# Two attention layers on one core: inverses written and read back in separate steps, mask loads, one accumulation and two norm operations moved

## The chip, the cores and the metric

The kernel runs on one core of a Trainium2 chip. The metric is the device time in microseconds (us) of one execution; of several executions the median is taken. The engines are called as the profile calls them: PE (TensorE matmul; PEld its weight loads), DVE (VectorE), ACT (ScalarE), POOL (GpSimd) and SP (SyncE, which here only issues DMAs). Each works through its own instructions in program order and waits where an operand is not ready.

## The reference

Sixteen batches of 1024 rows of 256 numbers pass through two masked-attention layers, each with a residual. All is float32; the adjacency is int32, with about 3% ones.

```python
h = jnp.maximum(_layernorm(x, axis=-1), 0.0)
x = x + _L0_gnn_ref(h, adj, ...)      # 4 heads of 64
h = jnp.maximum(_layernorm(x, axis=-1), 0.0)
x = x + _L1_gnn_ref(h, adj, ...)      # 8 heads of 32, with biases
# in each layer, for every head:
scores = q @ k.T * scale
attn = softmax(where(adj != 0, scores, -inf))
heads = attn @ v                      # concatenated, then @ Wo.T + bo
```

The layer norm takes the mean and the variance of each row: (x - m) / sqrt(v + eps).

## The kernel before

**Steps.** The attention is a stream of 768 steps. One step covers one quarter of a group's work in layer 0 (two heads, two blocks of 128 keys, 512 queries; four steps a group) or one eighth in layer 1 (four heads, one block of keys; eight steps a group). A group is half of the heads for half of the queries (`qh`, `g`), so that a batch has four groups: 16 steps in layer 0, 32 in layer 1. The stream interleaves batches: 16 steps of layer 0 of batch b+1, then 32 of layer 1 of batch b. This unit of 48 steps is called a period here, period b, and its steps are places 0 to 47; place 0 is `a = first[b+1]` of the code, place 16 is `c = second[b]`. Places of 48 and over lie in the period after.

**One step** (`Stream.run`, line 517). PE makes the scores into two PSUM pairs of three (`scores`, line 429, matmuls on 437); two steps later it multiplies the exponentials with the values (`weigh`, 471). Between, DVE applies the mask and writes the tile `p` (453; two instructions a step), and ACT takes the exponential in place (459). In layer 1 the weighing is done at odd places for two steps together. The row sums of the softmax come from adding `p` tiles and then one multiplication with ones (`count`, 338, on PE). In layer 0 the tiles are added on DVE and POOL (`add_tiles`, 480 to 486). In layer 1 POOL adds the two tiles of a pair (572; `p` of odd steps has two buffers, so DVE waits if POOL is late), and DMAs that POOL issues add those sums (`accumulate`, 558, 1 MB each).

**What is put between.** `later(i, f)` registers work for step i; it is issued at the end of that step in each engine's queue, in the order of registration (`LARGE` ones last). A step number is thus only a position in a queue. It is not a time. `end_group` (596) registers, when a group is done (step i; place 25, 33, 41 and 49 for the four groups of layer 1, and 5, 9, 13, 17 for those of layer 0): `spread` (the row sums go from PSUM by ACT and then by small DMAs to 128 lanes, 357 and 370), `invert` (DVE reciprocal `vn`, 378; a DMA writes it to `vd` in DRAM, 380; two or four DMAs read it back, broadcast, to `inv`, 383, each waiting on SP until `vd` has landed), `normalize` (POOL multiplies the output `cat` with `inv`, 389), and after the second group `end_half` (output projection, residual and, in layer 1, storing x: 419, 424, 427).

**Masks.** Each batch has eight mask tiles of 128 rows. `Mask.load` (line 145) is a DMA that POOL issues into the one buffer `adj`; `flip` (151) is a transposing DMA that SP issues into the one buffer `adjT`; `put` (160) is an ACT instruction that packs it. In the code (lines 768 to 771) they stand at places i-6, i-3 and i, for i = 7, 12, 17, 22, 33, 37, 41, 45. A load waits on POOL for the turning before it, which reads `adj`.

**Norms.** `norms` (705) registers `stats` for half of the rows in two steps: DVE takes bn_stats and bn_aggr of two tiles at each (188, 189). After the fourth tile POOL makes `ve` (192), the power -1/2 of it (194), `less` (196) and their product (198), all of 128x4 elements; ACT then normalizes. In periods from b = 1 on, the second parts of `stats` stand at places 12, 20, 29 and 38. `place_blocks` (245) and `put_blocks` (238) are the DMAs, on SP, by which normalized rows are turned; `open_x` (132) loads x on SP at places 5 and 13.

Of the kernel before, what the change touches and what calls it, by code (L numbers as in the profile page):

```python
# [10 lines left out]
F32 = mybir.dt.float32  # L11
# [4 lines left out]
ALU = mybir.AluOpType  # L16
PSUM = bass.MemoryType.PSUM

P = 128
EPS = 1e-5  # L20
# [65 lines left out]
def fast_program(ctx, tc, a, w, loads, chk):  # L86
# [3 lines left out]
    nc = tc.nc  # L90
    x, adj, out = a["x"], a["adj"], a["out"]
# [9 lines left out]
    small = ctx.enter_context(tc.tile_pool(name="small", bufs=2))  # L101
# [69 lines left out]
    class Inputs:  # L171
# [7 lines left out]
        def stats(self, half, tiles=range(4)):  # L179
            n = f"{self.n}_{half}"  # L180
            if 0 in tiles:
                self.mv[half] = small.tile([P, 4, 2], F32, tag="mv", name=f"mv_{n}")
            mv = self.mv[half]
            for i in tiles:
                stats = small.tile(
                    [P, nc.vector.BN_STATS_DIM], F32, tag="stats", bufs=1, name=f"st_{n}_{i}"
                )
                nc.vector.bn_stats(stats, xs[self.b, half][:, i, :])
                nc.vector.bn_aggr(mv[:, i, :], stats)
            if 3 in tiles:  # L190
                ve = small.tile([P, 4], F32, bufs=1, tag="ve", name=f"ve_{n}")
                nc.gpsimd.tensor_scalar_add(ve, mv[:, :, 1], EPS)
                self.rstd[half] = small.tile([P, 4], F32, tag="rstd", bufs=3, name=f"rstd_{n}")
                nc.gpsimd.tensor_tensor(self.rstd[half], ve, w.mhalf, ALU.pow)
                less = small.tile([P, 4], F32, bufs=1, tag="less", name=f"less_{n}")
                nc.gpsimd.tensor_scalar_mul(less, mv[:, :, 0], -1.0)
                self.shift[half] = small.tile([P, 4], F32, tag="shift", bufs=3, name=f"shift_{n}")
                nc.gpsimd.tensor_mul(self.shift[half], less, self.rstd[half])

# [109 lines left out]
    class Group:  # L309
# [65 lines left out]
        def invert(self):  # L375

            vn = small.tile([P, self.n_f], F32, tag="vn", bufs=1, name=f"vn_{self.n}")
            nc.vector.reciprocal(vn, self.sn)
            vd = dram.tile([self.per, 512], F32, tag=f"vd{self.layer}", name=f"vd_{self.n}")
            nc.sync.dma_start(self.lanes(vd), vn)  # L380
            self.inv = work.tile([P, 512], F32, tag="inv", bufs=1, name=f"inv_{self.n}")
            for r in range(self.per):
                nc.sync.dma_start(
                    self.inv[r * self.D : (r + 1) * self.D, :], vd[r].partition_broadcast(self.D)
                )
# [111 lines left out]
    class Stream:  # L497
# [12 lines left out]
        def later(self, i, f, *args):  # L510
            self.due.setdefault(i, []).append((f, args))
# [48 lines left out]
        def count_steps(self, i, st):  # L560


            gr, j = st.gr, st.j
            if gr.hurry and j >= NT - 2:
                if st.last:
                    self.counted(i, gr)
                gr.count(st.p, False, st.last)
            elif j % 2:
                one = self.steps[i - LEAD - 1].p
                if not (gr.brief or gr.pairs) and j == 7:  # L570
                    self.accumulate(gr.two, gr.one)
                nc.gpsimd.tensor_add(one, one, st.p)  # L572
                if gr.pairs:
                    self.later(i + 2, gr.count, one, j == 1, st.last)
                elif j == 1:
                    gr.one = one
                elif j == 3:
                    self.accumulate(one, gr.one)
                    gr.one = one
                    if gr.brief:  # L580
                        self.later(i + 8, gr.count, one, True, False)
                elif gr.brief:
                    self.later(i + (6 if j == 5 else 4), gr.count, one, False, st.last)
                elif j == 5:
                    gr.two = one
                else:
                    self.later(i + (2 if gr.last else 3), self.accumulate, one, gr.two)
                    self.later(i + (4 if gr.last else 8), gr.count, one, True, True)

        def counted(self, i, gr):  # L590
# [5 lines left out]
        def end_group(self, i, gr):  # L596

            if gr.hurry:
                for f in (gr.spread, gr.finish, gr.inp.test):
                    self.later(i, f)  # L600
                return

            if gr.layer == 0:
                self.later(i + 4, gr.count_added)
                at = 4, 6, 8, 11
            else:
                at = (8, 12, 17, 19) if gr.qh == 0 else (8, 11, 14)
                if gr.pairs:
                    at = 2, 5, 7, 9
                elif gr.last:  # L610
                    at = 4, 7, 9, 11
            for k, f in zip(at, (gr.spread, gr.invert, gr.normalize)):
                self.later(i + k, f)
            if gr.last:

                k = 7 if gr.layer or gr.inp.b == 0 else 37
                self.later(i + k if gr.inp.b + gr.layer < B - 1 else len(self.steps) + 2, gr.inp.test)
            if gr.g == 1:
                self.later(i + at[3], gr.end_half)

    def open_w(n):
        for _ in range(n):
# [5 lines left out]
    mask, inp = masks[0], inputs[0][0]  # L628
# [74 lines left out]
    later = stream.later  # L703

    def norms(inp, half, *at, whole=False):

        for i, f in zip(at, (inp.stats, inp.stats, inp.norm, inp.norm)):
            rest = (whole,) if i in at[2:] else ()
            later(i, f, half, (0, 1) if i in (at[0], at[2]) else (2, 3), *rest)
        later(at[3] + 1, inp.add_bias, half)  # L710

    def half_inputs(inp, half, *at):

        for i, f in zip(at, (inp.turn, inp.k, inp.q, inp.values)):
            later(i, f, half)
# [13 lines left out]
    for t in range(NT):  # L729
        i = 5 + 2 * t  # L730
# [8 lines left out]
    for b in range(B - 1):  # L739
        mine, a, c = inputs[1][b], first[b + 1], second[b]  # L740
        if b == 0:

            norms(mine, 0, a + 5, a + 6, a + 8, a + 9, whole=True)
            half_inputs(mine, 0, a + 11, a + 12, a + 14, a + 14)
            norms(mine, 1, a + 13, a + 14, a + 15, c, whole=True)
            half_inputs(mine, 1, c + 1, c + 3, c + 6, c + 4)
        else:
            norms(mine, 0, a - 20, a - 19, a - 16, a - 15)
            block_inputs(mine, 0, a - 14, a - 12, a, a + 2, a + 8)
            norms(mine, 1, a - 14, a - 10, a - 8, a - 6)  # L750
            block_inputs(mine, 1, a, a + 6, c, c + 6, c + 2)
        for i, u in zip((0, 2, 4, 6, 8, 10, 12, 13), range(NT)):
            later(a + i, masks[b].second, u)
        if b + 2 < B:
            other, mask = inputs[0][b + 2], masks[b + 2]
            later(a + 5, open_x, b + 2, 0)
            later(a + 13, open_x, b + 2, 1)
            if b == 0:
                norms(other, 0, a + 14, a + 15, c + 2, c + 3)
                block_inputs(other, 0, c + 4, c + 5, c + 8, c + 16, c + 18)  # L760
                norms(other, 1, c + 3, c + 4, c + 6, c + 7)
                block_inputs(other, 1, c + 10, c + 11, c + 22, c + 26, c + 30)
            else:
                norms(other, 0, a + 10, a + 12, a + 13, a + 15)
                block_inputs(other, 0, c, c + 1, c + 8, c + 16, c + 18)
                norms(other, 1, c, c + 4, c + 5, c + 6)
                block_inputs(other, 1, c + 7, c + 8, c + 22, c + 26, c + 30)
            for i, t in zip((7, 12, 17, 22, 33, 37, 41, 45), range(NT)):
                later(a + i - 6, mask.load, t)
                later(a + i - 3, mask.flip, t)  # L770
                later(a + i, mask.put, t)
        else:
            last, e = inputs[1][b + 1], c + 32
            norms(last, 0, c + 5, c + 6, c + 8, c + 9)
            block_inputs(last, 0, c + 10, c + 11, c + 14, c + 16, c + 20)
            norms(last, 1, c + 13, c + 14, c + 16, c + 17)
            block_inputs(last, 1, c + 18, c + 19, c + 24, e + 6, e + 4)
            for u in range(NT):
                later(c + 8 + 2 * u, masks[b + 1].second, u)
# [158 lines left out]
def kernel(  # L938
# [28 lines left out]
    with ExitStack() as fast, tc.manual_schedule():  # L967
        fast_program(fast, tc, a, w, loads, chk)
# [61 lines left out]
```

## Time and profile before

| what | us |
|---|---|
| median of 3 runs | 3355.89 |
| lowest and highest run | 3343.33, 3359.55 |
| the profiled execution, its own time | 3353.67 |
| its span, first to last instruction | 3351.9 |
| PE busy (96%) | 3228.7 |
| DVE busy (73%) | 2459.4 |
| POOL busy (70%) | 2349.5 |
| ACT busy (67%) | 2256.7 |

The mean clock granted to PE is 0.981 of full speed. In the profile a row such as "PE pz L338 <- DMA p<-p" reads: PE stood idle ahead of line 338, which writes `pz`, until the DMA from `p` to `p` had landed; then the total, the times and the longest. A timeline row gives start, length, engine, line, operation, `out<-in`, shapes and, in brackets, the idle time ahead of it. "SPq" is SP's issuing queue. A busy PE isn't PE at its peak, since the ends of matmuls are modelled.

### The profile page before, as it was taken

The page shows a single profiled execution, that of the slowest core. Times are in us where ns is not written, and L with a number is a line of the kernel's source. Part 1 is how long each engine was busy: PE and PEld are TensorE (multiplying, and loading weights), DVE is VectorE, ACT ScalarE, POOL GpSimd, SP SyncE. Part 2 cuts the span into 40 slices and gives each one's busy share as a digit, 9 for nine tenths or more (in the row PEclk, how much of TensorE's full clock was granted, in tenths as well). Part 3 has the DMA queues.
Part 4 walks back from the last instruction along what each step waited for, and adds up shares of the span by engine and source line. Part 5 has one row for each costly group of instructions (what it writes and reads, how often), then busy time and mean ns, then how long its engine had stood idle before and what let it go on. Part 6 is the DMA issues. An engine that isn't in the chain of part 4 may idle for free.

```text
span 3351.9 us, 43993 instructions
## 1 busy us (share of the span) xinstructions
PE 3228.7 (96%) x16302; PEld 1230.2 (37%) x16302; DVE 2459.4 (73%) x2658; ACT 2256.7 (67%) x2472; POOL 2349.5 (70%) x1274
## 2 busy tenths in 40 slices
PE   8999998999999999999999999899999999999998
PEld 3443333333333333333333334233333333333332
DVE  5677785877868778686877868678687786867766
ACT  5666675776767767676676766667677676766665
POOL 4567586685867758687685866767668686675776
PEclk9999999999999999999999999999999999999999
DMA  8348577494775948667485674956848577483441
GB/s 145 66 78 163 117 142 142 98 173 103 153 145 107 170 103 160 123 131 150 101 170 114 137 151 97 156 112 137 153 100 163 118 137 151 99 163 80 100 94 31
DMA packets 388063, 421.93 MB, mean 126 GB/s; under 512 B 197760, under 2 KB 324992, under 8 KB 365056
## 3 DMA queue, kind: packets, MB, share of 16 engines
q0 software_dynamic: 77856, 253.78, 42.7%
q1 hardware_dynamic: 309984, 165.26, 20.7%
q8 instruction: 130, 2.13, 0.3%
q14 instruction: 93, 0.76, 0.1%
HBM read 149.95 MB, written 47.96 MB: 59 GB/s over the span
## 4 chain that ended last, share of the span: by engine, by line
PE 68%; POOL 11%; DMA 9%; DVE 4%; issue 3%; ACT 2%; SPq 2%; POOLq 0%; DVEq 0%; ACTq 0%
PE ps L437 24%; PE po L471 20%; PE pq L263 10%; POOL p L572 8%; PE pv L299 6%; PE py L419 5%; DMA adjT<-adj 3%; DMA p<-p 3%; PE pz L338 3%; DVE p L453 3%; DMA vd<-vn 1%; SPq L370 1%; POOL p L483 1%; ACT p L459 1%; POOL p L558 1%
## 5 line engine op out<-in xcount | busy, mean ns | idle before, releaser
L453 DVE SCALAR_TENSOR_TENSOR p<-mask,ps 128x1024 f32<-128x1024 fp8e5 x1536 | 1794.4, 1215 | 635.5 <-PE ps L437 477.3
L459 ACT ACTIVATE p<-p 128x1024 f32<-128x1024 f32 x1536 | 1614.7, 1056 | 861.1 <-DVE p L453 817.3
L572 POOL TENSOR_TENSOR p<-p,p 128x2048 f32<-128x2048 f32 x255 | 1204.6, 4726 | 135.4 <-PE po L471 124.4
L437 PE MATMUL ps<-qT,kT 32*128 32x512 f32 (+1 forms) x6144 | 1220.5, 642 | 63.2 <-DVE p L453 58.8
L471 PE MATMUL po<-p,v 128*32 128x512 f32 (+1 forms) x6144 | 1002.5, 609 | 2.0 <-ACT cat L349 1.8
L437 PEld LDWEIGHTS ps<-qT,kT 32*128 32x128 f32 (+1 forms) x6144 | 386.3, 186 | 820.9 <-issue 405.4
L484 POOL TENSOR_TENSOR p<-p 128x1024 f32<-128x1024 f32 x128 | 302.2, 2361 | 296.6 <-DVE p L483 291.6
L471 PEld LDWEIGHTS po<-p,v 128*32 128x32 f32 (+1 forms) x6144 | 229.7, 118 | 705.1 <-issue 494.0
L483 POOL TENSOR_TENSOR p<-p 128x1024 f32<-128x1024 f32 x64 | 151.4, 2366 | 252.4 <-DVE p L480 166.4
L263 PE MATMUL pq<-hT,wk 128*128 128x512 f32 x512 | 242.7, 618 | 11.5 <-DMA hT<-turned 3.9
L263 PE MATMUL pq<-hT,wq 128*128 128x512 f32 x512 | 250.4, 634 | 0.1
L558 POOL DMA_DIRECT2D p<-p x178 | 178.1, 1001 | 96.3 <-DMA p<-p 49.3
L299 PE MATMUL pv<-wv,hT 128*128 128x256 f32 x1024 | 237.8, 385 | 0.0
L419 PE MATMUL py<-wo,cat 128*128 128x256 f32 x1008 | 233.5, 385 | 1.4
L299 PEld LDWEIGHTS pv<-wv,hT 128*128 128x128 f32 x1024 | 189.4, 190 | 71.3 <-issue 23.5
L419 PEld LDWEIGHTS py<-wo,cat 128*128 128x128 f32 x1008 | 186.6, 190 | 70.6 <-issue 42.9
L145 POOL DMA_DIRECT2D adj<-in_adj_dram x128 | 87.8, 688 | 133.9 <-DMA adjT<-adj 129.4
L389 POOL TENSOR_TENSOR cat<-cat,inv 128x512 f32<-128x512 f32 x127 | 175.0, 1378 | 6.1 <-DMA inv<-vd 4.3
L338 PE MATMUL pz<-p,ones 128*32 128x512 f32 (+1 forms) x888 | 148.7, 596 | 17.6 <-DMA p<-p 16.8
L160 ACT ACTIVATE mask<-adjT,numbers 128x1024 fp8e5<-128x1024 bf16 x124 | 140.8, 1136 | 34.3 <-DMA adjT<-adj 34.3
L480 DVE TENSOR_TENSOR p<-p 128x1024 f32<-128x1024 f32 x128 | 157.8, 1233 | 0.0
L486 POOL TENSOR_TENSOR p<-p,p 128x1024 f32<-128x1024 f32 x64 | 151.6, 2369 | 5.0
(51 smaller groups left out, 1600.7 us busy)
## 6 DMA issues: line engine op xcount, KB each, us to landing
p<-p POOLq DMA_DIRECT2D x178, 1024.0 KB, 9.5
adj<-in_adj_dram POOLq DMA_DIRECT2D x128, 256.0 KB, 4.4
x<-bo POOLq DMA_DIRECT2D x64, 512.0 KB, 6.4
turned<-hn SPq DMA_DIRECT2D x58, 512.0 KB, 3.5
hT<-turned SPq DMA_DIRECT2D x232, 128.0 KB, 4.2
x<-in_x_dram SPq DMA_DIRECT2D x128, 128.0 KB, 2.7
inv<-vd SPq DMA_DIRECT2D x128, 128.0 KB, 3.0
inv<-vd SPq DMA_DIRECT2D x252, 64.0 KB, 4.4
```

The source lines that it names most:

```text
L263: nc.tensor.matmul(pq[:, m, :], wt[self.layer][:, c, ts(m, P)], self.hT[half][:, c, :], start=(c == 0), stop=(c == 1),)
L299: nc.tensor.matmul(pv[:, i, :], self.hT[half][:, c, ts(i, P)], w.v[self.layer][:, c, :], start=(c == 0), stop=(c == 1),)
L338: nc.tensor.matmul(self.s[r * self.D : (r + 1) * self.D, :], w.ones.to_broadcast([P, self.D]), p[:, r, :], start=start, stop=stop,)
L419: nc.tensor.matmul(py[:, i, :], self.half.cat[:, c, ts(i, P)], w.o[self.layer][:, c, :], start=(c == 0), stop=(c == 1),)
L437: nc.tensor.matmul(st.ps[i // 2][:, i % 2, :], gr.inp.kT[r * D : (r + 1) * D, gr.g, ts(kt, P)], gr.inp.qT[gr.qh][r * D : (r + 1) * D, gr.g ...
L453: nc.vector.scalar_tensor_tensor(out=half, in0=gr.mask.m[gr.qh][:, kt, :].unsqueeze(1).to_broadcast([P, 2, 512]), scalar=-EDGE if gr.layer ...
L459: nc.scalar.activation(half, half, AF.Exp, scale=gr.scale)
L471: nc.tensor.matmul(gr.o[r * D : (r + 1) * D, :], gr.inp.v[:, kt, h * D : (h + 1) * D], st.p[:, i, :], start=(kt == 0), stop=(kt == NT - 1),)
L483: engine.tensor_add(b, two.p[:, 0:2, :], two.p[:, 2:4, :])
L484: nc.gpsimd.tensor_add(a, a, b)
L558: nc.gpsimd.dma_start(one, two, accum_op=ALU.add)
L572: nc.gpsimd.tensor_add(one, one, st.p)
```

## The change

Five edits. (1) Two POOL instructions of `stats` become DVE instructions that read `mv` twice. (2) `invert` is split: the reciprocal and the write of `vd` stay, the reading back becomes `fetch`, registered for a step of its own. (3) The last accumulation of a batch's last layer-1 group is registered for one step after the group's end (before: two). (4) The steps at which `spread`, `invert`, `fetch`, `normalize` and `end_half` are registered are set anew. (5) The mask loads are registered one step later.

```diff
             if 3 in tiles:
                 ve = small.tile([P, 4], F32, bufs=1, tag="ve", name=f"ve_{n}")
-                nc.gpsimd.tensor_scalar_add(ve, mv[:, :, 1], EPS)
+                nc.vector.scalar_tensor_tensor(
+                    out=ve, in0=mv[:, :, 1], scalar=EPS, in1=mv[:, :, 1],
+                    op0=ALU.add, op1=ALU.max,
+                )
+                less = small.tile([P, 4], F32, bufs=1, tag="less", name=f"less_{n}")
+                nc.vector.scalar_tensor_tensor(
+                    out=less, in0=mv[:, :, 0], scalar=-2.0, in1=mv[:, :, 0],
+                    op0=ALU.mult, op1=ALU.add,
+                )
                 self.rstd[half] = small.tile([P, 4], F32, tag="rstd", bufs=3, name=f"rstd_{n}")
                 nc.gpsimd.tensor_tensor(self.rstd[half], ve, w.mhalf, ALU.pow)
-                less = small.tile([P, 4], F32, bufs=1, tag="less", name=f"less_{n}")
-                nc.gpsimd.tensor_scalar_mul(less, mv[:, :, 0], -1.0)
...
             nc.sync.dma_start(self.lanes(vd), vn)
+            self.vd = vd
+
+        def fetch(self):
+
+            vd = self.vd
             self.inv = work.tile([P, 512], F32, tag="inv", bufs=1, name=f"inv_{self.n}")
             for r in range(self.per):
                 nc.sync.dma_start(
...
-                    self.later(i + (2 if gr.last else 3), self.accumulate, one, gr.two)
+                    self.later(i + (1 if gr.last else 3), self.accumulate, one, gr.two)
                     self.later(i + (4 if gr.last else 8), gr.count, one, True, True)
...
-                at = 4, 6, 8, 11
+                at = 4, 6, 7, 9, 11
             else:
-                at = (8, 12, 17, 19) if gr.qh == 0 else (8, 11, 14)
+                at = (8, 12, 14, 17, 19) if gr.qh == 0 else (8, 11, 12, 14)
                 if gr.pairs:
-                    at = 2, 5, 7, 9
+                    at = 2, 5, 6, 7, 9
                 elif gr.last:
-                    at = 4, 7, 9, 11
-            for k, f in zip(at, (gr.spread, gr.invert, gr.normalize)):
+                    at = 4, 6, 7, 9, 11
+            for k, f in zip(at, (gr.spread, gr.invert, gr.fetch, gr.normalize)):
                 self.later(i + k, f)
...
-                self.later(i + at[3], gr.end_half)
+                self.later(i + at[4], gr.end_half)
...
-                later(a + i - 6, mask.load, t)
+                later(a + i - 5, mask.load, t)
                 later(a + i - 3, mask.flip, t)
```

## The prediction

> **What bounds the kernel now.** The page comes first: how much idle time of PE is there at all.
>
> ```profile
> PE 3228.7 (96%) x16302; PEld 1230.2 (37%) x16302; DVE 2459.4 (73%) x2658; ACT 2256.7 (67%) x2472; POOL 2349.5 (70%) x1274
> ```
>
> PE is busy for all but 123 us. That, and time at half clock (clock 0.981: about 64 us lost), is all that an edit can win. Next, who ends PE's waits:
>
> ```profile
> PE ps L437 <- DVE p L453: 58.8, 36, 6.9
> PE pz L338 <- DMA p<-p: 16.8, 16, 2.6
> ```
>
> The rest is start and end. Placed by step (a step starts with its scores in PE's timeline), both sit at fixed places: the second at place 5 of periods 1 to 14, the first at places 42 and 44 of nearly every period. There DVE waits for POOL (`p` of odd steps), and POOL and SP wait as follows; the three lines are from the waits of all engines and of SP:
>
> ```profile
> DVE p L453 <- POOL p L572: 152.3, 92, 8.3
> POOL adj L145 <- DMA adjT<-adj: 129.4, 31, 9.6
> SPq L383 <- DMA vd<-vn: 350.6, 127, 11.2
> ```
>
> From here on I use period 4 (places 0 to 47: 955.4 to 1159.0 us), since steps agree between periods within 0.02 us at nearly all places outside 36 to 47.
>
> **The last accumulation: -16 us.** Timeline of POOL, then of PE, at places 3 to 5:
>
> ```profile
> 978.65 2.37 POOL L484 TENSOR_TENSOR p<-p 128x1024 f32<-128x1024 f32 x1
> 980.96 0.86 POOL L558 DMA_DIRECT2D p<-p  x1
> ```
> ```profile
> 988.82 1.06 PE L338 MATMUL pz<-p,ones 128*32 128x512 f32 x8 [1.03 <-DMA p<-p]
> ```
>
> The DMA stands behind two adds of step 3, which wait for DVE until 976.2; it lands at 988.8 and PE waits 1.03. At place 2 it stands before them: POOL is free at 971.3, and what it must wait for (the accumulation before) landed at 971.28. It then lands near 981, 7 us early. PE is at its own pace for the next 23 places, so the time stays won: thirteen times about 1.05 and once 2.6, 16 us. Ends: 0 and -16.
>
> **Mask loads: 0.** A step is only a position in a queue. At 27, 31, 35, 39 nothing of POOL is registered between the old and the new position: same order, same waits. At places 1 and 11 a load passes nothing or four small norm operations. At 6 and 16 it falls behind two adds: in period 4 from 993.1 to about 1003.2, landing 4 us later (median 4.4) near 1007.5, where the turning now issues at 1006.6. `put` is three places on, over 10 us; without that cover ACT would wait for each us.
>
> **`fetch` apart from `invert`.** On SP this matters only where something stands between. At 45/47 and in layer 0, except place 24, nothing does; at 24 one `put_blocks` passes (0.6 us). At place 5 `open_x` passes ahead of the reading back; it waits for the stored x until 990.9, the reads go then, and `normalize` needs them at 1003.2: nothing. The earlier reciprocal (place 7) comes to DVE at 998.3, and its sums landed at 997.6: nothing; exposed, at most 1 us a period. The place that counts is 37 to 39, where the turning of place 38 now comes ahead of the reads:
>
> ```profile
> 1122.80 1.34 SPq L380 DMA_DIRECT2D vd<-vn  x1
> 1130.19 2.40 SPq L383 DMA_DIRECT2D inv<-vd  x4
> 1132.69 1.34 SPq L151 DMA_TRANSPOSE adjT<-adj  x1
> ```
> ```profile
> 1137.61 0.66 POOL L145 DMA_DIRECT2D adj<-in_adj_dram  x1 [5.98 <-DMA adjT<-adj]
> ```
>
> The turning can issue at 1124.2 instead of 1132.7. That isn't the gain: POOL's accumulation issued at 1124.22 fills the DMA engines until 1135.7, and the next turning (place 42), queued behind such an accumulation, landed 0.8 to 1.1 us after it in twelve of fourteen periods. So I put the new landing 0.8 after that accumulation, or 1.4 after `vd` where this is later: 1136.5 for 1137.0. Over periods 0 to 13 the differences are 0.9, 3.6, 1.0, 0.6, 0.5, 0.7, 0.5, 1.0, 0.8, 2.4, 0.8, 0.9, 0.9 and 3.5: 18 us, which the chain load, add (572), mask (453), scores passes on to PE one for one. Ends: 0, and -60 if the turning slips through before the accumulation (then a good 4 of POOL's 6 us go each time).
>
> **Two norm operations on DVE.** POOL loses 0.22 + 0.24 us and two gaps, 0.58 a norm; after place 38 a wait for the turning eats it, elsewhere POOL has slack: -2 (0 to -8). On DVE each would cost about 0.2 (line 285, the same operation on small tiles, 0.18 at best), hidden nearly everywhere. But the trace has that operation on two SBUF operands beside a POOL add; DVE, then POOL:
>
> ```profile
> 1001.00 3.56 DVE L285 SCALAR_TENSOR_TENSOR chk<-sums,chk 128x64 f32<-128x64 f32 x2
> ```
> ```profile
> 1000.89 2.35 POOL L484 TENSOR_TENSOR p<-p 128x1024 f32<-128x1024 f32 x1
> 1003.21 1.26 POOL L389 TENSOR_TENSOR cat<-cat,inv 128x512 f32<-128x512 f32 x1
> ```
>
> Two operations of 0.2 us took 3.56; each ended 0.08 us after POOL's. [...] The new operations read `mv` twice, so they are such; bn_aggr has one input and took 0.18 beside the same adds. [...] At place 20: nothing. At 12: 1.1 us of an add left, DVE ahead of PE by more. At 38: 1.2 to 3.9 us left, but the next mask operation waits for the same add. At 29, DVE, then POOL:
>
> ```profile
> 1092.91 0.18 DVE L189 BATCH_NORM_AGGREGATE mv<-st 128x2 f32<-128x6 f32 x1
> 1093.01 5.73 DVE L453 SCALAR_TENSOR_TENSOR p<-mask,ps 128x1024 f32<-128x1024 fp8e5 x5
> ```
> ```profile
> 1090.58 4.56 POOL L572 TENSOR_TENSOR p<-p,p 128x2048 f32<-128x2048 f32 x1 [1.29 <-PE po L471]
> ```
>
> `ve` would go at 1095.2, `less` at 1095.4, the mask operation at 1095.6 instead of 1093.0. Five of these follow without a gap, behind them ACT and all of PE's queue: PE starts the second half of the scores of place 31 at 1094.3, as the first of them ends. So PE stands for 2.6 us, in fourteen periods (2.05 of the add left in each): +36. Ends: 0 and +37.
>
> **The clock.** In windows of 3.4 us, an isolated wait of 2.6 us at place 5 of period 8, and what followed (PE busy first, PEclk third from the end):
>
> ```profile
> 1801.70:1805.10 3.40, 1.23 (x10) 0.39 (x12) 0.12 (x1) 1.24 (x3) 3.11 (x2) 1.00 0.66 193
> 1805.10:1808.50 3.40, 3.40 (x10) 0.89 (x10) 1.23 (x2) 1.00 (x2) 2.12 (x2) 0.50 0.54 127
> ```
>
> [...] The trace decides otherwise: cutting it into the 3.41 us stretches in which the granted clock changes, of 16 at full clock with PE busy under 59% fourteen were followed by half clock, of 856 over 90% none. A 2.6 us stall leaves one stretch under or at about 62%. Half clock for 3.41 us costs up to 1.7; I take 1.2 a period: +17 (0 to +24).
>
> **Two small ones.** With PE 3.8 us later at place 31, POOL, which is late at place 35 in periods 9 to 13, catches up: -6 (0 to -12). The first period's norms lie in other places, with 1.1 to 1.3 us of a POOL operation left: +2 (0 to +6).
>
> **Sum.** -16 - 18 - 2 + 36 + 17 - 6 + 2 = +13, on the profiled execution's 3353.7: 3366.7. The median of the runs lies 2.2 above that execution, so 3369.
>
> **Rivals.** *The wait isn't there* (two reads of one tile, or of so few elements, go past POOL): +36, +17, -6, +2 fall away, -36: 3320. Against it speak 30 stretched operations of line 285. *The split gives nothing, slower*: the turning of place 38 lands no sooner, because the accumulation delays it fully and the reads queue behind it as before; place: POOL's wait on 145 at places 42 to 44; price: the 18 us; it decides from a landing 1.5 us after that accumulation, where the gain is gone. Then +31: 3387. For it speaks that in nine periods the gain is only 0.5 to 0.9 us. *The turning slips through*: 42 better than the forecast, 3327; against it, the twelve turnings that did not.
>
> **How the numbers follow.** About 0.5%, 17 us, is what a measurement of this kernel can tell from no change: under 3339 is faster, over 3373 slower. Forecast 0.46 (own range 3350 to 3386, a third of it slower), no wait 0.19 (nearly all faster), split gives nothing 0.27 (most of it slower), slipping through 0.08 (mostly faster). Faster 0.24, same 0.40, slower 0.36. The range, 3314 to 3394, leaves out the outer halves of the extreme cases, 0.2.
>
> **What would show it.** In the profile after: no wait of PE at place 5, for `p<-p` on 338; DVE's new operations in lines 192 to 200 with a median far over 0.2 us at places 29 and 38, ending with an add of 572; a wait of PE for 453 near 2.6 us at place 31 and half clock after it; the turning of place 38 issued ahead of the reads and landing just behind the accumulation; POOL's waits on 145 at 42 to 44 about 1 us shorter; loads at 27, 31, 35, 39 in the same order. I am wrong if those DVE operations take 0.2 us, or if POOL's wait there falls to nothing.

## The result, and the profile after

The changed kernel takes 3360.36 us (median of 20 runs, 3348.81 to 3378.97), the kernel before in the same comparison 3352.14 us (20 runs, 3339.18 to 3363.42). The ratio is 1.0029, with a 95% interval from 1.0014 to 1.0044: slower by 8 to 10 us, less than the 0.5% that the forecast took for what can be told from no change. The forecast of 3369 was 1.0039 of the median it started from. The small sum hides large terms. Without the norm edit the same kernel takes 3303 us (first experiment), so one edit gave away about 57 us and the others won about 49.

The page after, section 1 (busy time of the engines):

```profile
PE 3221.9 (96%) x16302; PEld 1225.2 (36%) x16302; DVE 2514.4 (75%) x2786; ACT 2254.8 (67%) x2472; POOL 2317.3 (69%) x1146
```

DVE has 128 more instructions and 55 us more; at 0.15 us each they would have been 19. POOL has 128 fewer and 32 us less. The waits of the engines after:

```profile
POOL p L583 <- PE po L482: 190.7, 119, 8.4
DVE p L464 <- POOL p L583: 110.3, 61, 15.3
POOL adj L145 <- DMA adjT<-adj: 99.3, 22, 15.3
PE ps L448 <- DVE p L464: 90.5, 34, 13.9
```

PE's wait for the mask operation rose from 58.8 to 90.5 us; its wait on `pz` for the DMA (16.8) no longer appears. 13.9 of the 90.5 are one wait, at place 44 of period 1, behind a turning that landed 21.9 us after its issue. POOL waits less for the turnings (99.3, was 129.4) and more for PE (190.7, was 124.4): POOL is less often the late one. The granted clock fell from 0.981 to 0.974; times the spans, 64 us lost before and 87 now.

**Place 29.** Period 4, timeline of DVE, of POOL and of PE:

```profile
1107.48 0.18 DVE L189 BATCH_NORM_AGGREGATE mv<-st 128x2 f32<-128x6 f32 x1
1107.70 2.02 DVE L192 SCALAR_TENSOR_TENSOR ve<-mv 128x4 f32<-128x4 f32 x1
1109.64 0.15 DVE L197 SCALAR_TENSOR_TENSOR less<-mv 128x4 f32<-128x4 f32 x1
1109.71 2.34 DVE L464 SCALAR_TENSOR_TENSOR p<-mask,ps 128x1024 f32<-128x1024 fp8e5 x2
```
```profile
1105.16 4.54 POOL L583 TENSOR_TENSOR p<-p,p 128x2048 f32<-128x2048 f32 x1 [1.29 <-PE po L482]
```
```profile
1107.83 1.13 PE L448 MATMUL ps<-qT,kT 32*128 32x512 f32 x4
1110.98 1.56 PE L448 MATMUL ps<-qT,kT 32*128 32x512 f32 x4 [2.02 <-DVE p L464]
```

`ve` takes 2.02 us and ends 0.02 after POOL's add (1109.72 against 1109.70). `less`, of the same form, takes 0.15; by then nothing of POOL runs beside it. Behind them the mask operation starts at 1109.71, and PE stands for 2.02 us between the halves of one step's scores. What the clock then does stands in windows of 3.4 us over the same stretch (PE busy first, PEclk third from the end):

```profile
1104.00:1107.40 3.40, 3.40 (x32) 0.80 (x32) 3.33 (x6) 1.99 (x2) 2.24 (x1) 1.00 0.89 170
1107.40:1110.80 3.40, 1.56 (x12) 0.30 (x4) 3.33 (x5) 0.12 (x1) 3.10 (x3) 1.00 1.12 208
1110.80:1114.20 3.40, 3.22 (x12) 0.50 (x12) 3.40 (x4) 3.10 (x3) 3.32 (x4) 0.61 1.13 175
1114.20:1117.60 3.40, 3.40 (x14) 1.25 (x11) 1.25 (x2) 1.13 (x2) 3.08 (x2) 0.50 0.99 207
```

One window with PE busy 46% is followed by two near half clock; the records have 6.83 us of it here.

**Where the time went.** A step's length runs from the start of its scores to the start of the next one's. Summed over 15 periods, against the profiled execution before (us; one execution each; places 40 to 47 scatter by some 5 us, as e1 and e10 show, which differ by the mask loads alone):

| kernel | places 5, 6 | 31 to 33 | 35 to 39 | 40 to 47 | all |
|---|---|---|---|---|---|
| changed kernel | -18.7 | +49.5 | -11.1 | -15.0 | +8.9 |
| e1, norms on POOL | -18.7 | +0.2 | -10.5 | -20.5 | -54.5 |
| e2, norms alone | -0.4 | +56.2 | -7.7 | -11.5 | +38.1 |
| e3, accumulation alone | -18.7 | +1.5 | +17.4 | +5.4 | +3.4 |
| e4, split alone | -11.4 | +0.3 | -10.3 | -17.6 | -35.4 |
| e5, loads alone | +0.2 | +1.3 | +6.4 | +1.5 | +12.7 |
| e6, one operand | -18.7 | +50.3 | -11.1 | -16.3 | +7.5 |
| e7, place 29 on POOL | -18.7 | +0.2 | -11.0 | -13.4 | -42.1 |
| e8, split, but not at 39 | -11.0 | +0.3 | -10.6 | -5.9 | -30.9 |
| e9, reduction | -18.7 | +3.7 | -10.9 | -16.7 | -41.4 |
| e10, split and accumulation | -18.7 | +0.3 | -10.7 | -25.3 | -54.4 |
| e11, e10 and reduction | -18.7 | +3.7 | -11.1 | -16.1 | -39.0 |
| e12, e11, POOL kept busy | -18.7 | +3.7 | -10.9 | -24.8 | -50.3 |

What is left to the whole is start, end, place 24 of period 0 and place 30 of period 14. The last took 4.7 us in e1, e3 and e8 and 10 to 12 in all others, whatever was edited: there PE waits for a projection whose last `hT` transfer, issued 0.5 to 1.6 us behind an accumulation, lands either with it or some 5 us before it. So e1 has 6 to 7 us over most kernels that no edit is known to have won; whether its other executions have them too was not seen.

### The profile page after: what moved, and what is told of

Read it like the earlier page. It is cut to its first block, busy times and chain, and to the rows that moved or that the text cites. A ratio compares the mean times of both kernels' runs of the same rounds, so it can differ in the third digit from the quotient of the medians.

```text
span 3360.8 us, 44052 instructions
## 1 busy us (share of the span) xinstructions
PE 3221.9 (96%) x16302; PEld 1225.2 (36%) x16302; DVE 2514.4 (75%) x2786; ACT 2254.8 (67%) x2472; POOL 2317.3 (69%) x1146
## 4 chain that ended last, share of the span: by engine, by line
PE 84%; DMA 6%; POOL 4%; DVE 3%; issue 1%; ACT 1%; SPq 0%; POOLq 0%; DVEq 0%; ACTq 0%
PE ps L448 30%; PE po L482 25%; PE pq L269 12%; PE py L430 7%; PE pv L305 7%; POOL p L583 4%; DMA adjT<-adj 3%; PE pz L344 3%; DVE p L464 2%; DMA p<-p 1%; ACT p L470 0%; ACT mask L160 0%; DMA vd<-vn 0%; DMA hT<-turned 0%; POOL p L569 0%
## 5 line engine op out<-in xcount | busy, mean ns | idle before, releaser
L583 POOL TENSOR_TENSOR p<-p,p 128x2048 f32<-128x2048 f32 x255 | 1195.1, 4689 | 201.5 <-PE po L482 190.7
L448 PE MATMUL ps<-qT,kT 32*128 32x512 f32 (+1 forms) x6144 | 1214.2, 649 | 92.6 <-DVE p L464 90.5
L482 PE MATMUL po<-p,v 128*32 128x512 f32 (+1 forms) x6144 | 1013.4, 617 | 1.8 <-ACT cat L355 1.6
L269 PE MATMUL pq<-hT,wq 128*128 128x512 f32 x512 | 239.6, 611 | 0.0
L269 PEld LDWEIGHTS pq<-hT,wk 128*128 128x128 f32 x512 | 94.9, 195 | 159.9 <-issue 114.7
L355 ACT COPY cat<-po 128x512 f32<-128x512 f32 x128 | 74.0, 578 | 117.8 <-PE po L482 117.7
```

What stands on the lines that cost most here:

```text
L269: nc.tensor.matmul(pq[:, m, :], wt[self.layer][:, c, ts(m, P)], self.hT[half][:, c, :], start=(c == 0), stop=(c == 1),)
L448: nc.tensor.matmul(st.ps[i // 2][:, i % 2, :], gr.inp.kT[r * D : (r + 1) * D, gr.g, ts(kt, P)], gr.inp.qT[gr.qh][r * D : (r + 1) * D, gr.g ...
L482: nc.tensor.matmul(gr.o[r * D : (r + 1) * D, :], gr.inp.v[:, kt, h * D : (h + 1) * D], st.p[:, i, :], start=(kt == 0), stop=(kt == NT - 1),)
```

## The experiments

Times are medians; ratios are to the kernel before, with 95% intervals. In the comparisons the kernel before had medians of 3351.4 (e1 to e8), 3355.8 (e9 to e11) and 3353.4 us (e12).

### e1: the norms back on POOL

```diff
-                nc.vector.scalar_tensor_tensor(out=ve, ...)
-                nc.vector.scalar_tensor_tensor(out=less, ...)
+                nc.gpsimd.tensor_scalar_add(ve, mv[:, :, 1], EPS)
+                nc.gpsimd.tensor_scalar_mul(less, mv[:, :, 0], -1.0)
```

> The changed kernel with the two norm operations back on POOL; the other three edits stay. Theory (DVE's first new operation waits for POOL's add at place 29, PE stands 2 us for it in 14 periods and loses clock behind it): the 49.5 us that places 31 to 33 took more fall away, some 8 us of POOL's catching up come back, so about 40 us under the changed kernel, near 3319 us, 0.990 of the kernel before (0.987 to 0.993). Rival 1 (PE's stall at place 31 has another cause, such as the moved loads): 1.000 to 1.004, and the stall is still there. Rival 2 (what places 40 to 47 won rests on PE's delay at 31, which lets POOL catch up, not on the split of the fetch): the stall goes, but places 40 to 47 give their 15 to 26 us back, 0.994 to 0.998.

3303.47 us, 0.9853 (0.9824 to 0.9883). The stall at place 31 is gone and places 40 to 47 keep what they had won. Both rivals fall. From its waits:

```profile
PE ps L442 <- DVE p L458: 47.9, 32, 5.0
```

The norm edit costs 57 us on top of the others, 17 more than the theory's 40. In the two profiled executions 49.3 lie at places 31 to 33, 5.5 at 40 to 47 and 6.6 at place 30 of period 14. Measured against e10, which lacks the moved loads too and whose place 30 is as in the changed kernel, it is 54.

### e2 and e3: the norms alone, the accumulation alone

Each is the kernel before with that one edit of the diff.

> The kernel before with the two norm operations on DVE and nothing else. Theory: places 31 to 33 take 49.5 us more as in the changed kernel, POOL's relief and catching up give back about 8, so about 3394 us, 1.012 of the kernel before (1.010 to 1.015). Rival 1 (another edit makes the stall): 1.000. Rival 2 (POOL catches up while PE stands, which takes away the stalls of places 42 and 44): +25 or less, 1.007 or below, with places 40 to 47 shorter by 15 or more.

3391.29 us, 1.011 (1.0083 to 1.0138). The stall comes with this edit alone: +56.2 at places 31 to 33, and 19 back at places 35 to 47, where POOL, with a later PE, waits more for PE (192 us at its adds, before 124). Rival 2 had the right sign at 35 to 47, but not the size.

> The kernel before with only the last accumulation one place sooner in its queue. Theory: PE's wait at place 5 goes in 14 periods, 16 to 19 us, and nothing takes its place: about 3335 us, 0.995 of the kernel before. Rival (POOL's accumulation now stands ahead of two adds, DVE's waits for POOL grow, and PE waits a place later for what it had waited for at place 5): 0.999 to 1.002.

3333.47 us, 0.9943 (0.9921 to 0.9965). As the theory said, and place 5 shows it in all fourteen periods (6.50 us; before, 7.60 in most). Its profiled execution was among its slowest runs (3357.15), for a reason told at the end.

### e4 and e8: the split alone, and with the reads of place 39 put back

e4 is the kernel before with `fetch` and the new `at`. e8 is e4 with the line below, which puts the reads of place 39 (and those of 47) back behind their inversion:

```diff
-                at = (8, 12, 14, 17, 19) if gr.qh == 0 else (8, 11, 12, 14)
+                at = (8, 12, 12, 17, 19) if gr.qh == 0 else (8, 11, 12, 14)
```

> The kernel before with only the reading back apart from the inversion. Theory (the turning of place 38 issues 8 us sooner and lands about 1 us sooner on the mean, since the accumulation holds it): 10 to 18 us, 0.995 to 0.997. Rival 1 (the split gives nothing; places 40 to 47 were won by the relief of POOL): 0.999 to 1.001, with places 40 to 47 as before. Rival 2 (the turning comes a good 3 us sooner each time, which the relief of POOL has hidden in the changed kernel): 30 to 45 us, 0.987 to 0.991.

3310.73 us, 0.9868 (0.9842 to 0.9895): 41 us, by time rival 2. By place it is not. Only 17.6 us lie at places 40 to 47, as the theory had it; 11.4 lie at places 5 and 6 and 10.3 at 35 to 39, where nothing had been expected of the split. Timeline of SP's queue and of POOL in e4, period 4:

```profile
1115.32 1.35 SPq L380 DMA_DIRECT2D vd<-vn  x1
1116.84 2.82 SPq L151 DMA_TRANSPOSE adjT<-adj  x1
1124.06 3.13 SPq L388 DMA_DIRECT2D inv<-vd  x4
```
```profile
1116.57 0.85 POOL L563 DMA_DIRECT2D p<-p  x1 [0.30 <-POOL p L577]
1130.14 0.66 POOL L145 DMA_DIRECT2D adj<-in_adj_dram  x1 [6.19 <-DMA adjT<-adj]
```

The turning now stands ahead of the reads and issues 0.3 us after the accumulation, not 8.5. POOL still waits 6.19 us for it. The trace has the accumulation landing at 1128.5 and the turning at 1129.6. Over 14 periods the turning lands 1.1 us after that accumulation on the mean (before: 2.3), and the next load goes 20.32 us after the start of place 38 (before: 21.56). That is 1.24 us, fourteen times 17.

> The kernel with the split alone, but with the reading back of the group that is inverted at place 37 issued at once, as in the kernel before, so that the turning of place 38 queues behind it again; all other places keep the split. Theory: what the split alone won at places 5 and 6 stays (11 us, the reads out of the accumulation's way), what it won at 35 to 47 (18 us at 40 to 47, and 10 of a late POOL at 35 to 39) goes: 0.995 to 0.998. Rival 1 (the gain at 35 to 47 comes from elsewhere): 0.986 to 0.989 as the split alone. Rival 2 (only the turning of place 38 counts, the gain at place 5 is chance): 0.999 to 1.001, and PE's wait at place 5 is back at 1.1 us.

3323.03 us, 0.9931 (0.9903 to 0.996). With the turning behind the reads again, places 40 to 47 give back 11.7 of their 17.6 us (12 by the medians). Places 5, 6 and 35 to 39 keep all, so the gain there is no chance. The theory had put 35 to 39 among the losses, which is why the time lies below its range. At place 5 e4's waits show why:

```profile
PE pz L338 <- DMA p<-p: 6.3, 14, 1.7
```

Before, four reads of `inv` went out from place 4 on, beside the accumulation, which took 7.8 us in period 4. In e4 they go at place 6, and it takes 7.1. The wait of PE shrinks from 16.8 to 6.3 us. The sooner accumulation removes the same wait whole, so the two edits share those 11 us: 18 and 41 apart by the medians, 49 together (e10), where the plain sum is 59.

### e5: the mask loads alone

The kernel before with `a + i - 5` for `a + i - 6`.

> The kernel before with only the mask loads one place later. Theory (nothing of POOL stands between the places at most loads, and at the two where two adds do, the turning still comes in time): 0.998 to 1.002. Rival (the edits add up only if the loads cost something: fetch alone 0.987 and accumulation alone 0.994 make 0.981, and the changed kernel with its norms on POOL, which holds both and the loads, gave 0.985): +14 us, 1.003 to 1.005. The theory takes that difference for an overlap: fetch alone already took 11 of the 19 us of the wait at places 5 and 6.

3361.24 us, 1.0028 (1.0008 to 1.0049): slower, if barely. But e1, which holds the loads, and e10, which does not, are equal (0.9853 and 0.9849). Beside the other edits they cost nothing that shows, but those two intervals are 17 to 20 us wide and do not exclude 10 us. No fixed place of e5's profile carries the 10 us; 6.6 lie at place 35 of period 9 (below). What the loads do there stays open.

### e6 and e9: two other forms of the norm operations on DVE

Both are the changed kernel with another form: e6 with one tensor operand, e9 as a reduction over one element, which leaves out the small constant.

```diff
-                nc.vector.scalar_tensor_tensor(out=ve, ...)
+                nc.vector.tensor_scalar_add(ve, mv[:, :, 1], EPS)                                 # e6
+                nc.vector.tensor_reduce(ve, mv[:, :, 1:2], mybir.AxisListType.X, ALU.max)         # e9
```

> The changed kernel with the two norm operations on DVE in a form with one tensor operand, tensor_scalar instead of scalar_tensor_tensor reading the same columns twice; results are the same numbers. Theory (what waits for POOL's add is the second SBUF input): the operation takes 0.2 us at place 29, places 31 to 33 fall back by 49 us, and POOL stays relieved: 3296 to 3305 us, 0.983 to 0.987. [...] Rival 2 (the operations' mere presence ahead of the mask operation costs 0.4 us of PE and half clock behind it): 0.990 to 0.995.

3360.96 us, 1.0032 (1.0018 to 1.0046): nothing changed, against the theory. One operand waits like two: the longest `ve` takes 2.026 us, in the changed kernel 2.025. This left open whether every DVE operation waits there.

> The changed kernel with the two norm operations on DVE as tensor_reduce over one element (the second with its sign turned); the small constant added to the variance is left out. [...] Rival (any DVE operation that comes after bn_aggr and writes a tile that POOL read waits for POOL): 2.0 us again, 1.001 to 1.005.

3317.8 us, 0.989 (0.9869 to 0.9911), a little over the 0.982 to 0.987 that had been expected if this form doesn't wait. The wait is gone. The operation by its line (shortest, median, longest in ns), in the changed kernel, in e6 and in e9:

```profile
L192 DVE SCALAR_TENSOR_TENSOR ve<-mv x64: 161/1064/2025, 7.8 to 3165.5; 128x4 f32<-128x4 f32 x64
```
```profile
L192 DVE TENSOR_SCALAR ve<-mv x64: 169/1070/2026, 7.9 to 3165.4; 128x4 f32<-128x4 f32 x64
```
```profile
L192 DVE TENSOR_REDUCE ve<-mv x64: 156/157/158, 7.9 to 3116.6; 128x4 f32<-128x4 f32 x64
```

The minimum is alike, so all three do 0.16 us of work; two of them wait. Place 29 of period 4 in e9, DVE, POOL and PE:

```profile
1081.66 0.16 DVE L192 TENSOR_REDUCE ve<-mv 128x4 f32<-128x4 f32 x1
1081.74 0.15 DVE L194 TENSOR_REDUCE less<-mv 128x4 f32<-128x4 f32 x1
1081.80 4.61 DVE L460 SCALAR_TENSOR_TENSOR p<-mask,ps 128x1024 f32<-128x1024 fp8e5 x4
```
```profile
1079.12 4.55 POOL L579 TENSOR_TENSOR p<-p,p 128x2048 f32<-128x2048 f32 x1 [1.28 <-PE po L478]
```
```profile
1083.07 1.13 PE L444 MATMUL ps<-qT,kT 32*128 32x512 f32 x4 [0.15 <-DVE p L460]
```

The add is the same and runs on until 1083.67; DVE passes it three times. PE stands for 0.15 us. So the price of the wait is the changed kernel less e9: 45.8 us at places 31 to 33, 43 by the medians. Why a reduction passes POOL's add and the two other forms wait for it, no run shows.

### e7: only place 29 back on POOL

```diff
+                here = self.layer == 1 and half == 0 and 1 <= self.b < B - 1
+                (nc.gpsimd form where here, else the nc.vector form)
```

> The changed kernel with the two norm operations back on POOL only in the norm of place 29 (layer 1, first half, 14 of 64 norms); the other 50 norms keep them on DVE. Theory (only there PE hangs on DVE): as with all norms on POOL or a little better, 3295 to 3305 us, 0.983 to 0.986. Rival (the waits of DVE at the other places, 38 above all, cost too): 0.990 to 0.997, with a wait of PE left at another place.

3317.75 us, 0.9908 (0.9874 to 0.9941). Fourteen of 64 norms carry all of the stall: places 31 to 33 are at +0.2. Those at places 12 and 38 wait too (1.1 us, and 1.0 to 2.4), with no PE behind it. But e7 is 14 us over e1, which the theory had not allowed; the rival's mechanism does not fit either, for e9, where DVE waits nowhere, lies at the same 3318. In the profiled executions the difference is 12 us: 7 at place 30 of period 14, most of the rest at places 40 to 47.

### e10, e11, e12: what POOL's relief is worth

e10 is the kernel before with split and accumulation only. e11 is e10 with e9's reductions. e12 is e11 with POOL still doing its two operations into tiles that nobody reads:

```diff
+                nc.gpsimd.tensor_scalar_add(ve2, mv[:, :, 1], EPS)
                 nc.gpsimd.tensor_tensor(self.rstd[half], ve, w.mhalf, ALU.pow)
+                nc.gpsimd.tensor_scalar_mul(less2, mv[:, :, 0], -1.0)
```

> The kernel before with the split and the sooner accumulation, without the moved loads and without the norm edit. Theory (split and accumulation share 11 us at places 5 and 6, loads cost nothing): the same as the changed kernel with its norms on POOL, 0.983 to 0.987, near 3302 us. Rival (the loads cost 10 us here too, as they did alone): 0.980 to 0.983, near 3292 us.

3306.31 us, 0.9849 (0.9823 to 0.9874), as the theory had it.

> The kernel with the split and the sooner accumulation, and with the two norm operations on DVE as tensor_reduce (the small constant added to the variance left out). [...] Rival 1 (this form waits too): 1.000 to 1.004. Rival 2 (POOL's relief is worth nothing or brings its next operations into worse places at 42 and 44, as it looked with the norms of place 29 on POOL): 2 to 12 us over the kernel with split and accumulation alone.

3318.06 us, 0.9895 (0.9869 to 0.9921): rival 2, 12 us over e10, where 0 to 8 us under it had been expected of POOL's relief. PE's wait for the mask operation in e10 and in e11:

```profile
PE ps L442 <- DVE p L458: 38.5, 40, 3.0
```
```profile
PE ps L444 <- DVE p L460: 54.6, 38, 5.5
```

With POOL relieved the waits are fewer and longer: the longest goes from 3.0 to 5.5 us. The mean length of place 42 falls from 8.11 to 6.22 us and that of place 44 rises from 4.96 to 7.68.

> The kernel with split, sooner accumulation and the reductions on DVE, and in addition POOL still does its two old operations into tiles that nobody reads (the small constant added to the variance is left out of what is used). With POOL relieved that kernel was 12 us over the one with the operations on POOL, with more of PE's wait at place 44 and less at 42. Theory (it is POOL's coming sooner that merges the two waits into one longer one): with POOL's load as before the 12 us shrink to the 4 that place 31 shows, 0.984 to 0.987, and places 42 and 44 are as in the kernel with split and accumulation. Rival (it is the reductions' place on DVE, ahead of the mask operations): 0.988 to 0.991 as without the two operations.

3308.03 us, 0.9864 (0.9825 to 0.9902), within the theory's numbers: places 40 to 47 come back from -16.1 to -24.8 (e10: -25.3). The lengths of 42 and 44 do not return (6.39 and 7.07), so the theory is half right. The intervals of e11 and e12 overlap. That POOL's relief costs some 9 us is likely, not settled, and its way is open. That it gains nothing is what e11 shows against e10; e7 and e9 against e1 say no more than that, since half of the difference lies at place 30 of period 14.

The best of these are e1 and e10, 1.5% under the kernel before and 1.6 to 1.7% under the changed one.

## Why the prediction was right

Its mechanism, the sign of its large terms and its sum were right. Several terms were not, and they cancelled: the norm edit was put at +47 (36 + 17 - 2 - 6 + 2) and costs 57, the other edits at -34 and win 49. That these two misses, of 10 and of 15 us, point opposite ways is luck.

- **Last accumulation, -16.** -18.7 at places 5 and 6, nothing in its place. Right.
- **DVE behind POOL's add at place 29, +36.** Right place, cause and count. That the operations read `mv` twice isn't what counts: with one operand `ve` takes as long (e6). The wait is 2.02 us fourteen times, 28, not 2.6. The forecast gave each new operation 0.2 us of its own behind the add, and both the wait; only `ve` waited, and DVE's operations start 0.07 us after one another there (1109.64, 1109.71).
- **The clock, +17.** 49.5 - 28.3 leaves 21 us. In eleven of fourteen periods (0 to 13) half clock followed, for 3.41 us or twice that; in periods 7, 12 and 13 it didn't, and there the step lengthened by 2.1 us alone. In e9 it followed in none. Gaps of 2.02 us did it here.
- **The turning ahead of the reads, -18.** Lands 1.1 us behind the accumulation (forecast 0.8), and the next load goes sooner by 17 us in all; putting the reads back takes 12 away (e8). Right in cause, and in size as far as the scatter of 5 us tells. In the split alone no turning slipped through before the accumulation; in the changed kernel four did (periods 1, 4, 5 and 6, by 2 to 3 us), too few for that rival, and the one of period 1 was late all the same, 21.9 us after its issue.
- **The other positions of the split, 0.** Failed. "It waits for the stored x until 990.9, the reads go then, and `normalize` needs them at 1003.2: nothing" looked only at who needs the reads. What they no longer disturb was left out: 0.7 us of an accumulation that PE waits for, 11 us with period 8's longer wait. It did not change the sum, since the sooner accumulation takes that wait away anyhow.
- **POOL catching up, -6, at place 35.** The norm edit alone gains 7.7 us at places 35 to 39 (e2); 2.1 of it, in period 12, every other kernel has too, but 4.8 in period 9 are its own, so by itself the term holds. But the split alone gains 10.3 there (e4), and all edits together gain 11.1: beside the split the catching up adds next to nothing.
- **POOL relieved, -2 (0 to -8).** Most likely the wrong sign: e11 lies 12 us over e10, of which 3.5 are DVE's own place at 31 (e9 lies 14 over e1, but half of that is place 30 of period 14). The reason given, a wait for the turning eats it, explains a zero and not a loss.
- **Mask loads, 0.** Nothing shows beside the other edits; alone about +10 us, and why stays open.

Rival "the wait isn't there" falls with place 29 above and with e9, "the split gives nothing" with e4 and e8.

## What to carry to other kernels

Before a small operation moves to an idle engine, look at what runs on the neighbour at that moment and what stands behind the operation in its new queue: 0.16 us of work, moved to an engine with a quarter of its time free, cost 3.3 us each time, because a mask operation that PE hung on stood behind it. Cost each form of an operation by a row of that form: here a scalar operation and one with two operands waited alike (2.03 us at the longest, each), a reduction did not (0.16). Where two edits remove the same wait, count it once, and ask of every transfer that moves what it stops disturbing, too.

## What the runs showed of the hardware

In the profiled executions of all four kernels that read `inv` back at place 4 (the kernel before, e2, e3, e5), and in none of the ten others, the DMAs in flight at places 29 to 31 of period 9 were slow: the turning and the accumulation issued at place 31 landed after 16 to 25 us, where the same ones of period 8 took 7 to 11. In e3 those of period 10 were slow too (19 and 20 us). POOL of e3, period 9:

```profile
2111.76 4.53 POOL L572 TENSOR_TENSOR p<-p,p 128x2048 f32<-128x2048 f32 x1
2133.03 0.65 POOL L145 DMA_DIRECT2D adj<-in_adj_dram  x1 [16.74 <-DMA adjT<-adj]
```

This is 8.3 of the 10 to 11 us that every kernel with the split wins at places 35 to 39, and the +17 of e3. It may also be why the 22 runs each of e3 and e5 spread over 44 and 50 us, and the 22 of e6 over 28. Why it comes in those periods only, and whether it is the order of the reads, some 25 places earlier, that prevents it, wasn't settled.

The order of those reads isn't all of it. At places 38 and 39 of period 1 of the changed kernel a turning and an accumulation, issued within half a microsecond of each other, landed after 21.9 and 23.5 us; PE's longest wait, 13.9 us, is the price. In e6 the same two took 14 to 19 us in periods 1, 6 and 7. No other kernel had one over 14 us outside periods 9 and 10, once the first 32 steps were through.
